# A four-layer graph attention kernel: layer 2 multiplied with 32 targets of weights in each quarter of the array's columns

## The chip, the cores and the metric

The kernel runs on one core of a Trainium2 chip. The metric is the device time of one execution in microseconds (us), the median of several runs.

## The reference

4096 nodes with 256 features pass through four graph attention layers, each with the same adjacency matrix and each added to its input. Of the four only layer 2 is touched here; it has 4 heads of 64 features.

```python
def _L2_gnn_ref(x, W, a, adj_matrix):                    # W: 4 heads x 256 x 64
    xt = jnp.einsum('ni,hio->hno', x, W)
    src = jnp.einsum('hnf,hf->hn', xt, a[:, :out_f])
    dst = jnp.einsum('hnf,hf->hn', xt, a[:, out_f:])
    e = jax.nn.leaky_relu(src[:, :, None] + dst[:, None, :], NEG_SLOPE)
    mask = (adj_matrix > 0)[None, :, :]
    e = jnp.where(mask, e, -jnp.inf)
    attention = jax.nn.softmax(e, axis=2)
    h_prime = jnp.einsum('hij,hjf->hif', attention, xt)
    return h_prime.transpose(1, 0, 2).reshape(n, heads * out_f)
...
h = jnp.maximum(_layernorm(x, axis=-1), 0.0)
x = x + _L2_gnn_ref(h, L2_gnn_W, L2_gnn_a, adj)
```

The last product, attention times features, is the one whose form changes. The softmax's divisor is carried as a 65th column of the features, and the result is divided by it at the end.

## The kernel before, in words

The nodes make 32 tiles of 128. Nodes with low numbers have many neighbours and nodes with high numbers few. So for each layer the first tiles of targets are worked densely, against all 32 tiles of sources, and the other targets against a list of sources: the first 4 tiles of sources (`DP`) for all, and then `CAPS[T]` tiles of listed sources, whose rows of features GpSimd gathers from a table in memory (line 1231, tile `s_gg`) together with their masks.

A `Unit` is one such piece of work, with a plan of steps. In layer 2 there are one dense unit of 4 target tiles (512 targets), whose 128 steps are 32 tiles of sources by 4 heads, and 28 listed units of one target tile, whose steps take all 4 heads at once; the listed units have 4 + `CAPS[T]` steps each, 330 in all. `run` goes through one merged plan of the layers 1, 2 and 3: the steps of the dense unit are dealt out between the listed units (`over_tiles`), and each step goes through four stages at different places of the plan (`LEAD = (0, 2, 3, 6)`):

- `fetch` loads or gathers features and mask;
- `begin` lets ScalarE make the weights of two of the four heads (line 1019, listed units of layer 2);
- `weigh` lets VectorE make the weights of the other heads and apply the mask (lines 1033 and 1042). The weights are a tile `s_p` of sources by targets;
- `multiply` adds the product to accumulators in PSUM. For layer 2 this is `multiply_heads`, line 1096.

Behind the multiplies a queue of small pieces of work is emptied a little at each step (`pump`). In it are the end of a target tile (`end2`) and the next layer's rows (`node_rows` with the transposes at line 716 and the projections at line 748). A program scheduler orders the instructions of all engines but GpSimd, whose order is as written.

In `multiply_heads` the features are held as the array's weights, 65 columns for a head, and the attention weights move: 128 columns in a listed step, 512 in a dense one. The accumulators hold 65 features by targets: for a listed unit one bank with 4 heads, for the dense unit four banks, one for a head. `end2` therefore copies a target tile's sums to SBUF on ScalarE (`s_o`, lines 1151 and 1154), turns them with four transposes (`s_oT`, line 1158), and then VectorE takes the reciprocals of the divisors, multiplies, and adds the result to `x`. Everything is float32, and a multiply stands as two records in the profile.

`target_rows` makes a unit's target factors `s_grow` and takes its buffer by a tag; the second dense unit of layer 1 shares the tag `o` with the copies `s_o`.

## Time and profile before

| | |
|---|---|
| time, median of 3 runs | 1800.04 us (1794.2 to 1804.27) |
| span of the profiled execution, first to last instruction | 1779.3 us |
| what lies around the span, median less span | 20.7 us |
| mean granted TensorE clock | 0.974 |
| busy: TensorE, its weight loads, VectorE, ScalarE, GpSimd | 1650, 1380, 1317, 632, 966 us |
| layer 2's multiplies, first to last | 833.9 to 1351.1 us |
| matmul records in all, and those of line 1096 | 9268, 2896 |

The profile gives one execution. PE is TensorE's matmuls and PEld its weight loads, which run beside them; DVE is VectorE, ACT ScalarE, POOL GpSimd, SP the engine that issues most transfers. A group of instructions is given as line, engine, operation, output<-inputs, shape, count, busy time and mean duration of one. The start of a matmul is measured; its end is modelled, and matmuls are pipelined, so that two records overlap [...].

### The profile page before, as it was taken

The numbers are of one execution on the slowest core, as the hardware profiler recorded it, in microseconds if no ns is written. First come the engines' busy times: TensorE is split into PE (matmuls) and PEld (weight loads), VectorE is DVE, ScalarE is ACT, GpSimd is POOL, SyncE is SP. The second block draws the span as 40 slices with busy tenths as digits, with TensorE's granted clock in tenths as the row PEclk, the third lists the DMA queues.
The fourth block names the chain that finished last, engine by engine and source line by source line (L and its number), as shares of the span: only waits on it lengthen the run. The fifth ranks groups of instructions, "written<-read, shape, count | busy, mean of one in ns | idle before, by whom it ended". The sixth has DMA issues, their size and how long they took to land.

```text
span 1779.3 us, 29208 instructions
## 1 busy us (share of the span) xinstructions
PE 1650.3 (93%) x9268; PEld 1379.5 (78%) x9268; DVE 1317.1 (74%) x3908; ACT 632.4 (36%) x1915; POOL 965.5 (54%) x930
## 2 busy tenths in 40 slices
PE   6998899889989899788999999988889999999997
PEld 4887778678768688676578777788889888888885
DVE  6887899777754676556899888987785666677755
ACT  5630010120120232333476776888894011111101
POOL 9836666636535656653355544434461666554554
PEclk9999999989889999999999999999999999999999
DMA  8899778844254444543233333322342766565554
GB/s 273 283 317 282 228 243 262 274 124 125 61 144 138 132 121 140 153 122 106 83 98 87 93 83 98 87 79 86 101 114 83 208 198 184 171 181 170 170 144 130
DMA packets 152237, 274.70 MB, mean 154 GB/s; under 512 B 21423, under 2 KB 75340, under 8 KB 152076
## 3 DMA queue, kind: packets, MB, share of 16 engines
q0 software_dynamic: 45584, 130.39, 27.2%
q1 hardware_dynamic: 105656, 141.83, 24.8%
q8 instruction: 77, 1.26, 0.3%
q14 instruction: 84, 0.69, 0.1%
q10 hardware_dynamic: 836, 0.53, 0.1%
HBM read 231.76 MB, written 40.90 MB: 153 GB/s over the span
## 4 chain that ended last, share of the span: by engine, by line
PE 77%; DVE 8%; DMA 5%; ACT 3%; issue 3%; another core or an unknown queue 2%; POOL 1%; SPq 0%; DVEq 0%; ACTq 0%; POOLq 0%
PE s_acc L1071 44%; PE s_accm L1096 20%; PE s_pj L748 7%; DVE s_p L1033 2%; DMA s_gg<-table,idx 2%; PE idx_ps L900 2%; DMA s_raw<-in_adjT 2%; PE s_sT L967 2%; ACT s_p L1019 2%; DVE s_m L1325 2%; PE s_tp L716 1%; DVE seen L1332 1%; PE s_oT L1158 1%; DVE first L875 1%
## 5 line engine op out<-in xcount | busy, mean ns | idle before, releaser
L1231 POOL DMA_INDIRECT s_gg<-table,idx x715 | 760.2, 1063 | 726.9 <-PE s_acc L1071 226.9
L1033 DVE SCALAR_TENSOR_TENSOR s_p<-s_grow,s_gg,mlist 128x128 f32<-128x128 f32 x994 | 308.8, 344 | 132.6 <-PE s_acc L1071 58.5
L1071 PE MATMUL s_acc<-s_gg,s_p 128*128 128x257 f32 x1430 | 352.4, 389 | 12.4 <-DVE s_p L1033 8.8
L1071 PEld LDWEIGHTS s_acc<-s_gg,s_p 128*128 128x128 f32 x1430 | 267.8, 193 | 57.6 <-DVE s_p L1033 14.9
L1071 PE MATMUL s_acc<-g,s_p 128*128 128x257 f32 x1152 | 292.2, 396 | 19.7 <-DVE s_p L1033 12.4
L1071 PEld LDWEIGHTS s_acc<-g,s_p 128*128 128x128 f32 x1152 | 219.7, 198 | 56.3 <-DVE s_p L1033 16.0
L1033 DVE SCALAR_TENSOR_TENSOR s_p<-s_grow,pre,mpre 128x128 f32<-128x128 f32 (+1 forms) x576 | 188.7, 368 | 44.9 <-PE s_acc L1071 28.0
L1096 PE MATMUL s_accm<-s_p,s_gg 128*65 128x128 f32 x1744 | 206.8, 274 | 1.8 <-issue 1.6
L1071 PE MATMUL s_acc<-s_gs,s_p 128*128 128x257 f32 x896 | 203.4, 380 | 0.4 <-DVE s_p L1033 0.4
L1096 PEld LDWEIGHTS s_accm<-s_p,s_gg 128*65 128x65 f32 x1744 | 194.6, 139 | 5.7 <-issue 3.1
L1019 ACT ACTIVATE s_p<-s_grow,s_minus,s_gg 128x128 f32<-128x128 f32 x436 | 185.9, 486 | 29.2 <-PE s_accm L1096 19.5
L1033 DVE SCALAR_TENSOR_TENSOR s_p<-s_grow,s_gs,s_ms 128x512 f32<-128x512 f32 x224 | 161.8, 746 | 46.5 <-PE s_acc L1071 20.3
L1071 PEld LDWEIGHTS s_acc<-s_gs,s_p 128*128 128x128 f32 x896 | 169.4, 190 | 25.6 <-DVE s_p L1033 1.6
L1071 PE MATMUL s_acc<-pre,s_p 128*128 128x257 f32 x768 | 184.9, 385 | 3.9 <-issue 2.0
L748 PE MATMUL s_pj<-s_w,s_hT 128*128 128x259 f32 (+3 forms) x640 | 169.0, 405 | 14.5 <-ACT s_hT L718 4.4
L973 ACT ACTIVATE s_grow<-s_sT 128x256 f32<-128x256 f32 (+2 forms) x136 | 46.8, 367 | 361.7 <-PE s_sT L967 239.3
L1071 PEld LDWEIGHTS s_acc<-pre,s_p 128*128 128x128 f32 x768 | 144.6, 193 | 27.4 <-issue 3.7
L748 PEld LDWEIGHTS s_pj<-s_w,s_hT 128*128 128x128 f32 x640 | 124.2, 201 | 42.5 <-ACT s_hT L718 7.6
L929 POOL DMA_INDIRECT mlist<-mask_t,idx x105 | 121.7, 1159 | 63.8 <-issue 30.9
L1096 PE MATMUL s_accm<-s_p,pre 128*65 128x128 f32 (+1 forms) x928 | 121.4, 286 | 1.9 <-issue 1.9
L1096 PEld LDWEIGHTS s_accm<-s_p,pre 128*65 128x65 f32 x928 | 105.2, 139 | 18.7 <-issue 16.1
L1019 ACT ACTIVATE s_p<-s_grow,s_minus,pre 128x128 f32<-128x128 f32 x224 | 96.3, 487 | 22.4 <-issue 16.6
(126 smaller groups left out, 1739.1 us busy)
## 6 DMA issues: line engine op xcount, KB each, us to landing
s_raw<-in_adjT SPq DMA_DIRECT2D x128, 512.0 KB
s_gs<-table SPq DMA_DIRECT2D x28, 516.0 KB
s_gg<-table,idx POOLq DMA_INDIRECT x715
mask_t<-s_m SPq DMA_DIRECT2D x35, 256.0 KB
table<-s_g SPq DMA_DIRECT2D x28, 258.0 KB
s_ms<-mask_t SPq DMA_DIRECT2D x28, 256.0 KB
table<-s_m SPq DMA_DIRECT2D x21, 256.0 KB
table<-g SPq DMA_DIRECT2D x8, 516.0 KB
```

What stands on the lines that cost most here:

```text
L716: nc.tensor.transpose(tp[:, c, :], zs[k][:, c * P : (c + 1) * P], ident)
L748: nc.tensor.matmul(ps, lhsT=hT[:, c, :], rhs=L.w[:, c, k * (D + 6) : k * (D + 6) + cols], start=(c == 0), stop=(c == 1),)
L900: nc.tensor.matmul(ps[:, 0:cap], lhsT=first[:, :, j % half], rhs=val[:, 0:cap, j * IT + t], start=(j == 0), stop=(j == JT - 1),)
L929: nc.gpsimd.indirect_dma_start(out=mlist[:, OFFS[T] + k, :], out_offset=None, in_=mask_t[T // IT], in_offset=bass.IndirectOffsetOnAxis(ap= ...
L967: nc.tensor.transpose(ps[:, h - h0, it, :], L.s[:, T0 + it, h : h + 1].to_broadcast([P, P]), ident)
L973: nc.scalar.activation(grow[:, h1:h2, :], ps[:, h1 - h0 : h2 - h0].rearrange("p h a b -> p h (a b)"), AF.Exp, scale=scale,)
L1019: nc.scalar.activation(w[:, h, :], u.grow[:, h, :], AF.Relu, scale=g[h][:, n - 1 : n], bias=minus)
L1033: nc.vector.scalar_tensor_tensor(p[:, k, :], u.grow[:, h, :], g[k][:, n - 1 : n], m, op0=ALU.min if L.l == 3 and h == 1 else ALU.max, op1= ...
L1071: nc.tensor.matmul(u.accs[it][h], lhsT=p[:, k, it * P : (it + 1) * P], rhs=g[k][:, 0:n], start=first, stop=last,)
L1096: nc.tensor.matmul(u.regions[h], lhsT=g[k][:, 0 : DH + 1], rhs=p[:, k, :],  start=first and (u.nt > 1 or h == 0), stop=last, skip_group_ch ...
L1231: nc.gpsimd.indirect_dma_start(out=wide, out_offset=None, in_=L.table, in_offset=bass.IndirectOffsetOnAxis(ap=index[T][:, k : k + 1], axis=0),
L1325: nc.vector.tensor_scalar(m[:, h * half : (h + 1) * half, :], raw, 0.0, None, op0=ALU.is_gt)
```

## The change

The roles of the two operands are exchanged. The attention weights `s_p` become the array's weights, 32 targets at a time, and each group of 32 is placed in its own quarter of the array's columns, since the output's partitions begin at 0, 32, 64 or 96 (the built instructions carry a tile of 128 rows by 32 columns at these positions). A head's 65 columns of features move. One multiply becomes 4 in a listed step (16 for its 4 heads instead of 4), and 16 in a dense head step instead of 1. The accumulators are targets by heads by features: one bank for each target tile, four for the dense unit. `end2` reads the accumulator directly: the copy and the transposes are gone, and the sum into `x` is put off by one turn of the queue. The second dense unit of layer 1 gets a buffer tag of its own.

```diff
+COLS = 32
...
         grow = (L.big if big else L.pool).tile(
-            [P, L.H, w], F32, name=f"s_grow_{L.l}_{T0}", tag=big or "grow", bufs=None if big == "growb" else 2
+            [P, L.H, w], F32, name=f"s_grow_{L.l}_{T0}", tag=big or "grow", bufs=None if big else 2
         )
...
         def multiply_heads(u, heads, g, p, first, last):
-            w = u.nt * P
-            if first and u.nt == 1:
-                t = ps_acc.tile([DH + 1, HEADS, w], F32, name=f"s_accm_2_{u.T0}", tag="acc")
-                u.accs = [t]
-                u.regions = [t[:, h, :] for h in range(HEADS)]
-            elif first:
-                if heads[0] == 0:
-                    u.accs = []
-                t = ps_acc.tile([DH + 1, w], F32, name=f"s_accm_2_{u.T0}_{heads[0]}", tag="acc")
-                u.accs.append(t)
-                u.regions = u.accs
-            for k, h in enumerate(heads):
-                nc.tensor.matmul(
-                    u.regions[h],
-                    lhsT=g[k][:, 0 : DH + 1],
-                    rhs=p[:, k, :],
-                    start=first and (u.nt > 1 or h == 0),
-                    stop=last,
-                    skip_group_check=True,
-                )
+            if first and heads[0] == 0:
+                u.accs = [
+                    ps_acc.tile([P, HEADS, DH + 1], F32, name=f"s_acch_{u.T0 + it}", tag="acc")
+                    for it in range(u.nt)
+                ]
+            for it in range(u.nt):
+                for k, h in enumerate(heads):
+                    for c in range(0, P, COLS):
+                        nc.tensor.matmul(
+                            u.accs[it][c : c + COLS, h, :],
+                            lhsT=p[:, k, it * P + c : it * P + c + COLS],
+                            rhs=g[k][:, 0 : DH + 1],
+                            start=first and h == 0,
+                            stop=last,
+                            skip_group_check=True,
+                        )
...
     def end2(u, it, T):
-        big = layers[2].big
-        o = big.tile([DH + 1, HEADS, P], F32, name=f"s_o_{T}", tag="o", bufs=2)
-        if u.nt == 1:
-            nc.scalar.copy(o, u.accs[0])
-        else:
-            for h in range(HEADS):
-                nc.scalar.copy(o[:, h, :], u.accs[h][:, it * P : (it + 1) * P])
-        yield 1.0
-        tp = ps_mm.tile([P, HEADS, DH + 1], F32, name=f"s_oT_{T}", tag="mm")
-        for h in range(HEADS):
-            nc.tensor.transpose(
-                tp[:, h, :], o[:, h, :], ident[0 : DH + 1, 0 : DH + 1]
-            )
-        yield 3.0
+        acc = u.accs[it]
         rz = small.tile([P, HEADS], F32, name=f"s_rz_2_{T}", tag="rz4")
-        nc.vector.reciprocal(rz, tp[:, :, DH])
-        y = big.tile([P, HEADS, DH], F32, name=f"s_y2_{T}", tag="y2", bufs=2)
+        nc.vector.reciprocal(rz, acc[:, :, DH])
+        y = layers[2].big.tile([P, HEADS, DH], F32, name=f"s_y2_{T}", tag="y2", bufs=2)
         nc.vector.tensor_tensor(
-            y, tp[:, :, 0:DH], rz.unsqueeze(2).to_broadcast([P, HEADS, DH]), op=ALU.mult
+            y, acc[:, :, 0:DH], rz.unsqueeze(2).to_broadcast([P, HEADS, DH]), op=ALU.mult
         )
+        yield
         nc.vector.tensor_add(x[:, T, :], x[:, T, :], y.rearrange("p h o -> p (h o)"))
         stored[T] = 2
...
-                    big="o" if ib else "growb",
+                    big="growc" if ib else "growb",
```

## The prediction

> **What bounds the kernel now.** I read the busy tenths of the 40 slices first, then the chain of work that ended last, then one stretch for itself.

> ```profile
> PE   6998899889989899788999999988889999999997
> DVE  6887899777754676556899888987785666677755
> ACT  5630010120120232333476776888894011111101
> ```
> ```profile
> PE s_acc L1071 44%; PE s_accm L1096 20%; PE s_pj L748 7%; DVE s_p L1033 2%; DMA s_gg<-table,idx 2%; PE idx_ps L900 2%; DMA s_raw<-in_adjT 2%; PE s_sT L967 2%; ACT s_p L1019 2%; DVE s_m L1325 2%; PE s_tp L716 1%; DVE seen L1332 1%; PE s_oT L1158 1%; DVE first L875 1%
> ```

> Layer 2 is line 1096: its multiplies run from 831 to 1351 us, slices 19 to 31. There TensorE (PE) stands at 9 in eight slices and at 8 in the other five, and 20% of the whole chain is this one line. The busy times of that stretch (us, then instructions in brackets; the columns are named in the first line):

> ```profile
> core 0: us, PE busy (x) PEld busy (x) DVE busy (x) ACT busy (x) POOL busy (x), PEclk, DMA share, GB/s
> 831.00:1351.00 520.00, 497.74 (x3490) 405.90 (x3489) 443.04 (x1396) 379.25 (x1055) 234.62 (x218) 0.99 0.33 90
> ```

> PE is idle for 22 us of 520 at a clock of 0.99; VectorE (DVE) has 77 us to spare, ScalarE (ACT) 141, GpSimd (POOL) 285. The waits of the stretch name PE as the one waited for:

> ```profile
> POOL s_gg L1231 <- PE s_accm L1096: 116.1, 61, 42.6
> DVE s_p L1033 <- PE s_accm L1096: 38.3, 50, 2.4
> ACT s_p L1019 <- PE s_accm L1096: 24.2, 40, 2.9
> ```

> So what line 1096 costs on PE passes nearly one for one into the end time, while a saving on PE is worth at most about 77 us before DVE takes over.

> **The prices.** The busy time of a matmul is modelled and overlaps the next, so I use the distance from start to start: in a merged row of n equal matmuls, (length minus one duration) / (n-1). The rows (start us, length us, ..., count):

> ```profile
> 10.83 0.24 PE L640 MATMUL s_pb<-s_av,s_bc 128*1 128x2 f32 x4
> ...
> 543.27 1.94 PE L580 MATMUL s_wa<-s_av,s_wt 64*128 64x2 f32 x16
> ...
> 999.78 2.35 PE L1096 MATMUL s_accm<-s_p,s_gg 128*65 128x128 f32 x20
> 1001.97 3.60 PE L1096 MATMUL s_accm<-s_p,s_gs 128*65 128x512 f32 x8
> 1005.40 0.41 PE L1158 MATMUL s_oT<-s_ident,s_o 65*128 65x65 f32 x4
> ```

> The means of one are in the groups by shape: 274 ns (128 moving columns), 592 (512), 233 (transpose), 249 (L580), 164 (L640).

> - 128 moving columns: (2350-273)/19 = 109 ns. 512: (3600-592)/7 = 430 ns. The slope is 321/384 = 0.836 ns a column, so 65 moving columns cost 109 - 63 x 0.836 = **57 ns** if matmuls stand in a row; the 65-column transposes of L1158 show (410-233)/3 = 59.
> - Weights: L580 moves 2 columns under 128 columns of weights: (1940-249)/15 = 113 ns, so 0.88 ns a column of weights, and 32 columns are about 28 ns.
> - The closest two matmuls with weights of their own stand anywhere: L640, (240-164)/3 = **25 ns**.

> A float32 multiply is two records: 1744 + 896 = 2640 passes in tiles of 128 targets for 330 steps of 4 heads (two ACT operations a step, 436 + 224, give the same 330), and 224 + 32 = 256 passes for the 128 head steps of the dense block. Layer 2 therefore holds PE for 2640 x 109 = 288 us and 256 x 430 = 110 us, 398 of the 520.

> [...]

> **The change part by part.**

> *The multiplies.* A listed step of 4 heads was 8 passes of 128 columns, 0.872 us. It becomes 4 heads x 4 quarters = 16 multiplies, 32 passes with 32 columns of weights and 65 moving. A dense head step was 2 passes of 512 columns, 0.860 us, and becomes 4 target tiles x 4 quarters = also 32 passes. Moving columns go from 1024 to 2080 a step: only overlap between the quarters can pay for that, and it isn't in the trace. The bounds of one multiply (two passes): the two passes of one quarter use the same columns of the array and follow each other in program order, so the second waits for the first, 57 ns, and holds up everything behind it. The next quarter can then join the running second pass. [...] I take 25, the closest distance that the trace shows with a weight load in between; two loads of 28 ns fit into the sum. So a multiply costs 57 + 25 = 82 ns, a step 16 x 82 = 1.31 us.

> Listed: 330 x (1.31 - 0.87) = +145 us. Dense: 128 x (1.31 - 0.86) = +58 us. Sum +203, all on PE, which has no cover but 22 us of idle time.

> *Changes of mode.* In the built order of instructions the new multiplies stand in about 102 blocks, separated by layer 3's projections and transposes (L748, L967, L716), so 204 changes. [...] I take 164: +33 us.

> *End of a tile.* The 128 transposes of L1158 go, 128 x 59 = -8 us on PE. The ACT copies at L1151 and L1154 (28 x 578 + 16 x 259 ns = 20 us) go too; ACT has 141 us free, so that is worth nothing. DVE keeps its reciprocal, product and sum, reading the accumulator in place of the transposed copy. The reciprocal now waits for the tile's last multiply on DVE's queue, where ACT's copy waited 17.9 us before. Behind it stand the weighting operations of the next steps; PE has about three weighted steps in hand (the leads 3 and 6), 3.9 us at 1.31, against DVE's 2 x 0.344 + 0.415 = 1.1 us a step. Nothing; without that cover 28 tiles x 1.1 = 31 us. The next layer's rows become ready a few us sooner, which nobody waits for.

> *Buffers and queues.* The accumulators stay at four banks for the dense block and one for a tile. POOL's instruction order is unchanged and it has 285 us free; its gathers wait on PE as before. On SP a few loads of a stream change places: nothing. The second dense block of layer 1 gets its own buffer: nothing, its neighbours were not used at that time.

> *Sum.* +203 + 33 - 8, minus 15 of the 22 us of idle time that a fuller PE swallows: +213. The profiled execution had a span of 1779 us; the median of the three runs is 1800, so 21 us lie around it. 1779 + 213 + 21 = **2013 us**, and PE alone bounds layer 2, which grows to about 733 us.

> **The rivals.**

> - *No overlap (serial).* The quarters follow each other at 57 ns a pass, because the tiles share a stream or because they are not treated as tiles. Step 32 x 57 = 1.82 us: 330 x 0.95 + 128 x 0.96 = +437, +33 - 8 - 15, so **2247 us**; with L1158's 59 it would be 2276. For it: every stream in the trace is strictly in a row. [...]
> - *Full overlap, faster.* If the passes of all quarters pack at L640's 25 ns, a step is 0.80 us: 330 x 0.07 + 128 x 0.06 = -31, -8 for the transposes; [...] **1761 us**. It decides from a multiply under 0.872 / 16 = 54 ns, which even one pass of 57 excludes unless the array lets a second quarter go ahead of the first one's second pass. DVE's 443 us would allow it.
> - *Loads no longer hidden.* If a load can't run beside a matmul on the same rows, a pass is 57 + 28 = 85 ns and a step 2.7 us: +850 us, **2650 us**. Against: in the trace all loads of the 65 weights are hidden behind passes of 109.

> **How the numbers follow.** Half overlap 0.52, serial 0.33, loads exposed 0.08, full overlap 0.07. [...] The range from 1840 to 2285 holds half overlap and serial, 0.85, less a little at both ends. About 0.5%, 9 us, is what a measurement of this kernel can tell from no change. Faster by more than that: full overlap, most of it, 0.05; within it: the meeting of that and cheap half overlap, 0.03; slower 0.92.

> **What would show it.** The groups of the new multiply line: some 14,650 passes of 128x65, and their distances: alternately 57 and 25 if right, 57 throughout if serial, 85 if loads stand free. [...] PE at 9 through all of layer 2 and DVE falling to about 6 shows that PE bounds. The forecast is wrong if PE falls below 9 there, or if DVE's reciprocal holds the chain.

## The result and the profile after

The change made the kernel slower on the chip where both were first compared: 1870.74 us (median of 4) against 1798.27 us (median of 4), a ratio of 1.0406 with a 95% interval of 1.0377 to 1.0436, so +72 us where +213 had been forecast. On a further chip, where the kernel before takes 1700 us, the same changed kernel was no slower: 0.9989 (0.9969 to 1.0009). Both numbers have to be explained; for the first that succeeds only in part.

The busy tenths of the changed kernel, first chip:

```profile
PE   6998898999998999787677777787877999999997
DVE  6888898777545675457776777777767467677765
ACT  5620020110211232233454555577776111111111
PEclk9999999999789999889888888889988999999999
```

Layer 2 now reaches from slice 19 to slice 31. PE has fallen from 8 and 9 to 6 to 8, and DVE and ACT have fallen too. No engine is full: something that is none of the three takes the time. The forecast had named this as a sign of its being wrong. The granted clock dips in the same slices (0.89 over the stretch from 844 to 1445 us). The waits of the stretch from 844 to 1445 us (engine and line, what it waited for, us in total, times, longest):

```profile
PEld s_acch L1093 <- issue: 190.7, 349, 2.5
PE s_acch L1093 <- issue: 127.5, 267, 2.3
POOL s_gg L1215 <- PE s_acch L1093: 121.9, 27, 41.5
```

"issue" is time in which the engine waited for nothing that the profile shows. Before the change the whole stretch held 55 us of it for the weight loads of line 1096. What the passes themselves cost stands in the groups by line:

```profile
L1093 PE MATMUL s_acch<-s_gg,s_p 128*32 128x65 f32 x6976 | 183.8, 238 | 78.2 <-issue 71.1
L1093 PEld LDWEIGHTS s_acch<-s_gg,s_p 128*32 128x32 f32 x6976 | 141.4, 119 | 119.1 <-issue 106.3
L1093 PE MATMUL s_acch<-s_gs,s_p 128*32 128x65 f32 x3584 | 93.4, 253 | 31.8 <-issue 31.2
L1093 PE MATMUL s_acch<-pre,s_p 128*32 128x65 f32 x4096 | 96.3, 235 | 28.0 <-issue 25.2
```

Together 14,656 passes with a busy time of 374 us where line 1096 had 421. The array does its part in less time than before. The timeline shows both sides of it (start us, length us, ..., count, idle time before):

```profile
986.10 0.78 PE L1093 MATMUL s_acch<-pre,s_p 128*32 128x65 f32 x40
...
1040.31 1.48 PE L1093 MATMUL s_acch<-s_gg,s_p 128*32 128x65 f32 x58
1042.21 0.35 PE L1093 MATMUL s_acch<-s_gg,s_p 128*32 128x65 f32 x4 [0.42 <-issue]
1042.98 0.28 PE L1093 MATMUL s_acch<-s_gg,s_p 128*32 128x65 f32 x3 [0.43 <-issue]
1043.71 0.77 PE L1093 MATMUL s_acch<-s_gg,s_p 128*32 128x65 f32 x35 [0.44 <-issue]
```

In the first row 40 passes stand (780-220)/39 = 14.4 ns apart, **four passes of 65 columns in 57 ns**, the estimate for a single one when they stand in a row: the four quarters run side by side. A step of 32 passes takes 0.46 us where the old one took 0.87. In the other rows, passes come three or four at a time, some 0.7 us from one small burst to the next, and the profile shows nothing that they waited for.

What else grew with the passes is in the transfers: the page's row for one queue before and after (packets, MB, share):

```profile
q8 instruction: 77, 1.26, 0.3%
```
```profile
q8 instruction: 168, 2.75, 0.6%
```

91 packets more of 16 KB. TensorE's records rose from 2 x 9268 to 2 x 20,900 (matmuls and loads), 23,264 more, and 23,264 / 91 = 256. So this queue, which the page calls "instruction", is taken to bring TensorE's instructions, 256 in a packet, and 128 passes use one up. The two runs further down with more passes still agree: small multiplies added has 14,656 more instructions than the changed kernel and 58 packets more, 32 columns with moving split 29,312 and 115. In layer 2 of the changed kernel 118 packets stand 5.07 us apart on average and never less than 3.38, while the array needs 128 x 14.4 ns = 1.8 us for 128 passes.

This gave theory A: TensorE is short of instructions. Its rival B: the gaps belong to the tiles themselves, changes of mode and waits between quarters.

### The profile page after: what moved, and what is told of

The parts are those of the page before. It is cut to its first block, busy times and chain, and to the rows that moved or that the text cites. A ratio compares the mean times of both kernels' runs of the same rounds, so it can differ in the third digit from the quotient of the medians.

```text
span 1868.9 us, 52567 instructions
## 1 busy us (share of the span) xinstructions
PE 1612.8 (86%) x20900; PEld 1333.3 (71%) x20900; DVE 1312.4 (70%) x3908; ACT 604.7 (32%) x1871; POOL 959.3 (51%) x930
## 5 line engine op out<-in xcount | busy, mean ns | idle before, releaser
L1073 PE MATMUL s_acc<-s_gg,s_p 128*128 128x257 f32 x1430 | 356.8, 392 | 10.8 <-DVE s_p L1035 9.2
L1093 PE MATMUL s_acch<-s_gg,s_p 128*32 128x65 f32 x6976 | 183.8, 238 | 78.2 <-issue 71.1
L1093 PEld LDWEIGHTS s_acch<-s_gg,s_p 128*32 128x32 f32 x6976 | 141.4, 119 | 119.1 <-issue 106.3
L750 PE MATMUL s_pj<-s_w,s_hT 128*128 128x259 f32 (+3 forms) x640 | 177.6, 416 | 15.1 <-ACT s_hT L720 7.1
L1093 PE MATMUL s_acch<-s_gs,s_p 128*32 128x65 f32 x3584 | 93.4, 253 | 31.8 <-issue 31.2
L1093 PE MATMUL s_acch<-pre,s_p 128*32 128x65 f32 x4096 | 96.3, 235 | 28.0 <-issue 25.2
```

What stands on the lines that cost most here:

```text
L750: nc.tensor.matmul(ps, lhsT=hT[:, c, :], rhs=L.w[:, c, k * (D + 6) : k * (D + 6) + cols], start=(c == 0), stop=(c == 1),)
L1073: nc.tensor.matmul(u.accs[it][h], lhsT=p[:, k, it * P : (it + 1) * P], rhs=g[k][:, 0:n], start=first, stop=last,)
L1093: nc.tensor.matmul(u.accs[it][c : c + COLS, h, :], lhsT=p[:, k, it * P + c : it * P + c + COLS], rhs=g[k][:, 0 : DH + 1], start=first and ...
```

## The experiments

All later runs came from three further chips, whose times of the kernel before agree (1699.5, 1700.1 and 1699.6 us), so their ratios can be compared. The lengths of layer 2 are from the first to the last start of its multiply line; the distances are those of the packets that start within it. A mean distance is what the layer drew, not what the queue could give: times the number of packets it is the layer's length by construction. The row "before" has layer 2 from the kernel's repeat on one of these chips.

| kernel | passes in layer 2 | packets there, mean distance | layer 2 | ratio to before (95%) |
|---|---|---|---|---|
| before | 2,896 | 28, 16.9 us | 492 us | 1 |
| changed, first chip | 14,656 | 118, 5.07 us | 600 us | 1.0406 (1.0377 to 1.0436) |
| changed, again | 14,656 | 118, 4.17 us | 494 us | 0.9989 (0.9969 to 1.0009) |
| 64 columns | 7,328 | 61, 7.35 us | 454 us | 0.9767 (0.9750 to 0.9783) |
| 128 columns | 3,664 | 33, 14.8 us | 494 us | 1.0033 (1.0011 to 1.0056) |
| quarter outermost | 14,656 | 119, 4.78 us | 568 us | 1.043 (one run) |
| 64 columns, moving split | 14,656 | 119, 4.70 us | 559 us | 1.0366 (1.0349 to 1.0383) |
| small multiplies added | 21,984 | 175, 3.99 us | 700 us | 1.1202 (1.1183 to 1.1222) |
| 32 columns, moving split | 29,312 | 232, 3.90 us | 908 us | 1.244 (one run) |
| 32 dense, 64 listed | 9,376 | 77, 5.93 us | 462 us | 0.9774 (0.9740 to 0.9808) |
| 64 dense, 32 listed | 12,608 | 103, 4.36 us | 450 us | 0.9759 (0.9732 to 0.9786) |
| 64 columns, again | 7,328 | 61, 7.34 us | 453 us | 0.9759 (0.9728 to 0.9790) |
| 64 columns, sum on GpSimd | 7,328 | 61, 8.52 us | 522 us | 1.0170 (1.0138 to 1.0202) |

**Halves of 64.**

```diff
-COLS = 32
+COLS = 64
```

> The changed kernel with COLS = 64: two halves of 64 targets in place of four quarters of 32, so half the multiplies (7,328 passes in place of 14,656). Theory A (PE is short of instructions: its stream of them is refilled in packets of 16 KB, 5.0 us apart on average in layer 2 of the changed kernel, and PE stands idle with the cause 'issue' for 318 us in front of the new line, while in undisturbed stretches four passes of 65 columns take 57 ns): two passes of different halves should take 57 ns, a step of 16 passes 0.46 us as before, with half the instructions; the idle time with the cause 'issue' falls to under 60 us, layer 2 becomes bound by VectorE's 440 us, and the kernel is faster than before the change: 1730 to 1765 us. Theory B (the gaps come with tiling itself, from changes of mode or from waits between tiles): the gaps stay, 1830 to 1880 us.

Measured: 1660.35 us against 1699.52, ratio 0.9767. The waits of line 1093 in layer 2 of this kernel, and the busy times:

```profile
PEld s_acch L1093 <- DVE s_p L1035: 29.8, 74, 1.2
PEld s_acch L1093 <- DVE s_p L1044: 21.4, 56, 1.5
```
```profile
core 0: us, PE busy (x) PEld busy (x) DVE busy (x) ACT busy (x) POOL busy (x), PEclk, DMA share, GB/s
786.00:1241.00 455.00, 427.35 (x7791) 336.93 (x7790) 427.39 (x1390) 350.34 (x1011) 258.32 (x218) 0.96 0.38 104
```

The weight loads now wait for VectorE's weights, "issue" in front of the line is down from 318 us to 10 (loads and multiplies added, so that a pause of both counts twice), and VectorE is busy for 427 of 455 us. The fastest 32 passes took 930 ns, two in 58 ns: the step of 16 passes costs as little as with quarters and half the instructions. The forecast in microseconds was for the first chip; as a ratio, 1730 to 1765 is 0.962 to 0.981, which holds 0.977. This is faster than both kernels. It fits A and contradicts B only as far as tiles of 64 share what tiles of 32 have.

**No tiles.**

```diff
-COLS = 32
+COLS = 128
```

> The changed kernel with COLS = 128: the operands exchanged, but no column tiles; 3,664 passes of 128 columns of weights and 65 moving. Both theories: no overlap of tiles, so a pass is bounded by its weight load, 111 to 113 ns for 128 columns as L580 showed, 8 x 112 = 0.90 us a step against 0.87 (listed) and 0.86 (dense) before: layer 2's multiplies 410 us against 398, less 8 us of transposes: 1790 to 1820 us, no change that can be told. If a load of 128 columns takes only as long as four loads of 32 side by side (57 ns), a step would be 0.46 us and the kernel at 1730 to 1765 us: then the tiles bring nothing of their own.

Measured: 1.0033, as both theories had it. In a row of the timeline (of this kernel) 34 passes stand (3960-275)/33 = 112 ns apart:

```profile
902.23 3.96 PE L1093 MATMUL s_acch<-s_gs,s_p 128*128 128x65 f32 x34
```

That is the distance at L580 of the kernel before, 113 ns with 128 columns of weights and only 2 moving, so the load sets it and not the 65 columns that move. Exchanging the operands alone brings nothing; the tiles bring the gain: one load of 128 columns takes the 112 ns, two passes with a load of 64 columns each took 58.

**The quarters outermost.**

```diff
-                for k, h in enumerate(heads):
-                    for c in range(0, P, COLS):
+                for c in range(0, P, COLS):
+                    for k, h in enumerate(heads):
```

> The changed kernel with the loops over quarters and heads exchanged: the four heads of one quarter follow each other, 8 passes on the same columns of the array, before the next quarter. Number of instructions and shapes as in the changed kernel. If passes overlap only with passes on other columns: 57 ns a pass inside a quarter, a listed step about 1.5 to 1.8 us in place of 0.46 (the dense steps, one head at a time, keep their order), 330 x 1.2 = +400 us at most in the array, of which the idle time of 318 us already covers most: 1900 to 2150 us. Theory A adds nothing here; if passes overlap whatever their columns, or if instructions alone set the pace, it stays at 1860 to 1880 us.

Measured in one run: 1772 us, 1.043 times the kernel before; layer 2 takes 568 us against 494 with the quarters innermost. "Issue" in front of the line falls to 73 us, and PE is busier, since a listed step now takes 1.04 us in the array, 32.5 ns a pass (median of 32 passes). A row of it, (5390-220)/156 = 33 ns:

```profile
955.92 5.39 PE L1093 MATMUL s_acch<-s_gg,s_p 128*32 128x65 f32 x157
```

If each quarter had to finish first a pass would take 57 (an estimate). So the order matters, but the passes don't stand wholly in a row: on average 57 / 32.5 = 1.75 run at once. As a ratio 1.043 is what was expected if the order were harmless (1860 to 1880 us are 1.034 to 1.045), but that expectation took the changed kernel's time from the first chip. The next set of runs puts the changed kernel at 1.00 on such a chip, so the 74 us are put down to the order.

**As many instructions in halves.**

```diff
-COLS = 32
+COLS = 64
...
+                    for a0, a1 in ((0, 33), (33, DH + 1)):
...
-                            rhs=g[k][:, 0 : DH + 1],
+                            rhs=g[k][:, a0:a1],
```

> COLS = 64, and each head's 65 moving columns in two multiplies of 33 and 32: as many instructions as the changed kernel (14,656 passes), in tiles of 64, and the same columns moved in all. Theory A (number of instructions): the idle time with the cause 'issue' comes back, 1840 to 1890 us as the changed kernel. Theory B (tiles of 32 themselves): like the run with COLS = 64.

Measured: 1.0366. The time came as A said, but for another reason, so this run doesn't decide. The timeline of this kernel:

```profile
903.36 2.82 PE L1094 MATMUL s_acch<-s_gg,s_p 128*64 128x33 f32 x90
```

(2820-223)/89 = 29.2 ns a pass, though only 33 columns move: two in 58 ns, as with all 65 moving. So the moving columns don't set the pace. The loads of 64 columns fit it (at the 0.88 ns a column of L580 an estimate of 56 ns for each, two side by side), and splitting the moving columns loads all weights twice. A step costs 0.93 us in the array, 427 us over 458 steps, and with about 100 us of other work PE is full; "issue" is only 26 us. The expectation had overlooked that.

**The changed kernel again**, beside the next three:

> The changed kernel as it is, beside the next three on one chip, since the time of the kernel before differs by 6% between the first measurement (1798 us) and the second (1700 us). Both theories: 1.035 to 1.045 times the kernel before; layer 2's new line spans 560 to 600 us.

Measured: 0.9989, against the expectation of both theories. Its timeline is the clearest view of the shortage:

```profile
880.12 1.11 PE L1093 MATMUL s_acch<-s_gs,s_p 128*32 128x65 f32 x64 [2.22 <-issue]
881.03 1.12 PE L1093 MATMUL s_acch<-pre,s_p 128*32 128x65 f32 x64
883.59 1.12 PE L1093 MATMUL s_acch<-pre,s_p 128*32 128x65 f32 x64 [1.44 <-issue]
884.51 1.12 PE L1093 MATMUL s_acch<-s_gg,s_p 128*32 128x65 f32 x63
887.34 2.41 PE L1093 MATMUL s_acch<-s_gg,s_p 128*32 128x65 f32 x126 [1.72 <-issue]
```

126 to 128 passes, then 1.4 to 2.2 us of nothing, and again: one packet of 256 instructions is 128 passes. A limit on each single instruction would spread the passes out; here up to 128 run with their loads 14 ns apart, and then none. The packets' own times in the trace tie the pauses to them. In layer 2 the distance from one start of a matmul to the next exceeds 1 us 76 times; 70 of these pauses end 1.1 to 1.7 us after a packet has landed, where a stretch of 0.6 us after each landing would catch 14% by chance. With halves of 64 there are 8 such pauses, and none ends there. That layer 2 takes 494 us, as in the kernel before (492), is a coincidence of the array's saving and the pauses.

**Small multiplies added.**

```diff
+            for j in range(EXTRA):                    # EXTRA = 8
+                c, it = j * COLS % P, j % u.nt
+                nc.tensor.matmul(
+                    u.accs[it][c : c + COLS, HEADS, 0:1],
+                    lhsT=p[:, 0, it * P + c : it * P + c + COLS],
+                    rhs=g[0][:, 0:1],
...
```

> The changed kernel with 8 more multiplies in each of the 458 steps of layer 2: 32 columns of weights, one moving column, into a PSUM column that nothing reads. Passes go from 14,656 to 21,984, moving columns by under 1%. Array time of the extra passes: 7 to 25 ns each, 16 a step, so 0.11 to 0.40 us a step on top of 0.46; with the 100 us of other work 360 to 490 us, under the 560 to 600 that layer 2 takes now. Theory A (the supply of instructions paces TensorE at 119 packets of 256 instructions, 4.7 to 5.0 us each): 7,328 passes more are 14,656 instructions, 57 packets, +270 us: 1.18 to 1.22 times the kernel before. Theory B (tiles, their changes of mode and their waits): the extra time is hidden in the gaps, 1.03 to 1.06.

Measured: 1.1202, far above B's 1.03 to 1.06 and below A's 1.18 to 1.22. Layer 2 grew from 494 to 700 us, +206 us for 57 packets, **3.6 us a packet**; A had said +270, with a packet's mean distance on the slower chip. Of 122 pauses over 1 us, 120 end 1.1 to 1.7 us after a packet has landed. Multiplies with a single moving column, which by the expectation's estimate (0.11 to 0.40 us a step) the array could have taken into its gaps, cost 12%.

**The moving columns split in quarters of 32.**

```diff
+                    for a0, a1 in ((0, 33), (33, DH + 1)):      # with COLS = 32
```

> COLS = 32 with the 65 moving columns in two multiplies of 33 and 32: 29,312 passes. Two questions. Pace: with 3.6 us for a packet of 256 instructions (the price from the run with small extra multiplies) 14,656 passes more are 114 packets, +410 us on the changed kernel: 1.22 to 1.27 times the kernel before. Array: in undisturbed stretches four passes of different quarters take about 28 ns if the moving columns set the 57 ns of the changed kernel, and 57 ns still if four weight loads of 32 columns set it; in that case layer 2's array time is 458 x 0.91 = 420 us, still below the supply.

Measured: 2114 us, 1.244, and layer 2 of 908 us: +414 us for 114 packets, again 3.6 us each, as expected from the run before. Two rows of it (of this kernel), and the two waits that head its layer 2:

```profile
902.88 1.98 PE L1094 MATMUL s_acch<-s_gg,s_p 128*32 128x33 f32 x127 [1.50 <-issue]
907.22 1.98 PE L1094 MATMUL s_acch<-s_gg,s_p 128*32 128x33 f32 x127 [2.35 <-issue]
```

```profile
PEld s_acch L1094 <- issue: 383.7, 254, 3.3
PE s_acch L1094 <- issue: 347.1, 205, 3.2
```

The next in size, VectorE's 315 us and ScalarE's 275, are waits for this line. The fastest 32 passes took 255 ns against 450 in the changed kernel, so with quarters it is the moving columns, not the loads, that set the 57 ns. The granted clock of the stretch is only 0.65, against 0.96 in the changed kernel; that doesn't explain the pauses, since all 190 that exceed 1 us end 1.1 to 1.7 us after a packet has landed.

**Mixed tiles.**

```diff
+                    cols = 32 if u.nt > 1 else 64     # and, in the second kernel, 64 and 32
```

> Quarters of 32 for the dense unit, halves of 64 for the listed units: 9,376 passes. Theory A: 76 packets of 4.7 us are 360 us, under VectorE's 440, so as fast as 64 everywhere: 0.975 to 0.985 times the kernel before. Theory B: the dense unit's share (128 of 458 steps) of the loss of tiles of 32 against 64, 0.28 x 6.4%: 0.99 to 1.0.

> Halves of 64 for the dense unit, quarters of 32 for the listed ones: 12,608 passes. Theory A: 103 packets of 4.7 us are 482 us against the 454 that layer 2 took with 64 everywhere, +30 us: 0.99 to 1.005 times the kernel before. Theory B: 0.72 x 6.4% on top of 0.977: 1.02 to 1.03.

Measured: 0.9774 and 0.9759. Both are as fast as 64 everywhere, though the second has quarters in 330 of 458 steps. For the first, A was right and B (0.99 to 1.0) was not. For the second both missed: B, which put the loss on tiles of 32, had 1.02 to 1.03, and A had 0.99 to 1.005 with its price of 4.7 us. With the 3.6 us found since, 103 packets are 371 us, below the time for which VectorE is busy in this layer:

```profile
784.00:1235.00 451.00, 371.90 (x13074) 304.63 (x13073) 427.60 (x1390) 348.57 (x1011) 269.70 (x218) 0.99 0.39 107
```

(The columns are those of the row for halves of 64.) The second kernel still has 44 pauses over 1 us, 70 us in all; they cost nothing that can be seen where VectorE has 428 us to do.

**The kernel before and halves of 64 once more, and the sum on GpSimd.**

> The kernel before, unchanged, to have its trace from the same chip as the others; the first pair came from a chip on which it took 1798 us, the later ones took 1700. If that difference lies in the engines' own issuing, ScalarE's and VectorE's idle time with the causes 'issue' and 'remote' (165 and 74 us in the first trace) is nearly gone here, as it is in the changed kernel's second trace (16 and 0.4 us), and layer 2's multiplies span about 490 to 500 us. If it lies in the clock or in the transfers, those stay and the durations differ.

> COLS = 64 once more, beside the next kernel: 0.973 to 0.981 times the kernel before, layer 2's new line over about 454 us.

> COLS = 64, and the sum into x at the end of a tile on GpSimd instead of VectorE: 32 operations of 417 ns leave VectorE, which was busy for 427 of the 455 us of layer 2. If VectorE bounds layer 2 with COLS = 64: -8 to -13 us, 0.968 to 0.974 times the kernel before. If GpSimd's fixed order holds its gathers back behind these sums (each waits for VectorE's product): +5 to +30 us, 0.98 to 0.995.

Measured: the kernel before took 1698.67 us, its layer 2 492 us, with PE busy for 490 of 495 us:

```profile
786.00:1281.00 495.00, 490.03 (x3490) 402.90 (x3489) 439.36 (x1394) 379.32 (x1054) 237.51 (x218) 1.00 0.35 95
```

ScalarE's "issue" is 13 us where the first chip had 146, and VectorE's "issue" and "remote" (a wait for a signal whose sender the profile doesn't show) together are gone where it had 74; the durations of operations agree. So on the first chip several engines stand idle without a visible cause, with either kernel. In the changed kernel most of TensorE's pauses there aren't those of theory A. Layer 2 has 198 distances of 0.6 to 1 us from start to start on the first chip, 130 us in all, against 17 and 13 us on the second; they are the gaps between the small bursts of the first timeline. Of the 198, 32 end 1.1 to 1.7 us after a packet has landed, hardly more than chance would give (12%). Pauses over 1 us are fewer there, 35 and 55 us in all against 76 and 130 us. What makes the short pauses, and why on that chip, wasn't settled. Halves of 64 gave 0.9759 again.

With the sum moved,

```diff
-        nc.vector.tensor_add(x[:, T, :], x[:, T, :], y.rearrange("p h o -> p (h o)"))
+        nc.gpsimd.tensor_add(x[:, T, :], x[:, T, :], y.rearrange("p h o -> p (h o)"))
```

the kernel lost, 1.0170, more than the bad case expected (0.98 to 0.995). The waits of its layer 2 say why:

```profile
POOL x L1152 <- DVE s_y L1148: 130.0, 25, 10.3
ACT s_p L1021 <- DMA s_gg<-table,idx: 77.7, 83, 4.0
```

GpSimd stands 130 us in its fixed order before sums whose product isn't there yet, the gathers behind them start late, and ScalarE then waits for gathered features. So this run doesn't decide whether VectorE alone bounds the kernel with halves of 64.

## Why the prediction was right or wrong

- **PE bounds layer 2 before: right.** On the further chips PE is busy for 490 of 495 us. The ceiling that DVE sets fits too: with halves of 64 layer 2 falls by 38 us, VectorE is then busy for 427 of 455, and the loads wait for its weights.
- **57 ns for a pass of 65 columns: right** as the pace of one quarter; the timeline gives four passes, as many as there are quarters, in 57 ns.
- **82 ns for a multiply: wrong, and this is the term that failed.** "The second waits for the first, 57 ns, and holds up everything behind it" was the author's assumption; the trace before has no tiled matmul. The runs show otherwise: with the two passes of a quarter one behind the other in the program, passes stood 14.4 ns apart, so a multiply costs 28.5 ns in the array, a step 0.456 us and not 1.31. Even with eight passes in a row on one quarter it was 32.5 ns each and not 57. The term of +203 us should have been 458 steps x 0.456 us less 398, **-189 us**.
- **Missing from the sum: the supply of instructions.** The forecast counted 14,656 passes and asked only what the array does with each. At 3.6 us for 128 passes the lasting pace is 28 ns a pass. At the forecast's own 41 ns (82 for two) the supply would have kept up, so the omission shows only because the array is faster than forecast; the rival of full overlap took the 25 ns of four passes at L640 for a pace that lasts. On the second chip the pauses for instructions return all of the gain (494 us against 492). On the first chip layer 2 takes 600 us against 517; there most of the pauses are the short ones, whose cause stays open.
- **Changes of mode: sized too high.** The 164 ns were the author's estimate. From the last tiled start to the next untiled one it is 150 ns (median), where a tiled pass takes 57 by the estimate. Back it is 202 ns behind a transpose and 309 behind a projection, where the kernel before has 109 and 216. That is 93 ns more each way, and 101 x 2 x 93 ns = 19 us where 33 were taken.
- **End of a tile and queues:** the transposes' 8 us were not measured apart. The kernel without tiles agrees with them: +12 us for passes of 112 ns, -8 for the transposes, +6 measured. VectorE did stand before its reciprocals waiting for line 1093, 7 us in all on the second chip and 23 on the first, where nothing was taken.
- **The rivals.** Serial and exposed loads are both excluded by 14.4 ns a pass. Full overlap was given 0.07 and was what the array did. What this rival lacked is the shortage of instructions; with half as many the kernel gains 39 us. That it had forecast the same size (1761, -39) is luck: it had it from a step of 0.80 us on PE, where a step takes 0.46 us and VectorE then sets the time.

The sign was right on the first chip by luck: the array did not slow down, and what took the time was not in the text. The size was three times too large.

## What to carry to other kernels

Before cutting multiplies into more and smaller ones, count instructions: where TensorE's instructions for a step (two to a pass) take longer to arrive (3.6 us for 256 here) than any engine takes for that step, the array's saving is lost, as it was here with quarters on the second chip (layer 2 494 us against 492). In the timeline this is seen as bursts of 128 passes with "issue" between, and in the page as packets of the instruction queue. Take the widest tile that still gives the overlap: here two halves of 64 do a step in the array in 0.465 us, four quarters of 32 in 0.456, with half the instructions for the halves. And measure on more than one chip before explaining a few per cent.
